# A graph network layer on one Trainium2 core: the source columns of one tile in every 11th group come from TensorE instead of a gather

## The chip, the core and the metric

The kernel runs on one core of one Trainium2 chip. The core has TensorE (PE; its weight loads are listed apart as PEld), VectorE (DVE), ScalarE (ACT), GpSimd (POOL) and SyncE (SP), which issues DMAs. SBUF is the working memory, PSUM the memory into which TensorE writes. The metric is the device time of one execution in microseconds; the time of a kernel is the median of its runs.

## What is computed

One layer of a graph network over 12500 nodes with 64 features and 212500 edges with 32 features. The edges are sorted by their target.

```python
msg_in = jnp.concatenate([nodes[row], nodes[col], edge_features], axis=-1)
messages = _mlp(msg_in, mW1, mb1, mW2, mb2)          # relu(x @ W1 + b1) @ W2 + b2
aggregated = jax.ops.segment_sum(messages, col, num_segments=nodes.shape[0])
upd_in = jnp.concatenate([nodes, aggregated], axis=-1)
return _mlp(upd_in, uW1, ub1, uW2, ub2)
...
x = _layernorm(x + _L0_gnn_ref(x, src, dst, edge_attr_32, ...), axis=-1)
```

Here row is src and col is dst. All numbers are float32.

## The kernel before

The edges go through in 554 groups of 384, a group being three tiles of 128 edges (TG = 3). Group g is worked on in three parts, each of which ends with instructions on other engines:

- *turn* (L373 on): the ring `own.s` holds for every edge of the group the 64 features of its source node and a one-hot row of 32 places, which says to which target in the group's window of 32 nodes the edge goes. Three TensorE transposes (L378) put this into the PSUM tile `ps[0]`, 96 rows by 384 columns. ACT copies it into the block `own.st` (L389), where the edge features have been loaded below it as rows 96 to 127.
- *hidden*: three matmuls (L404) of that block's columns with `wm`, which holds the weights for the source, the window's projected target rows and the weights of the edge features. VectorE applies the relu into `own.h` (L415).
- *sums*: three matmuls (L431) add up the hidden rows by target: the weights are `h`, the moving operand is the one-hot part, repeated TIMES = 4 times, so that 128 columns are streamed, of which the first 32 are used. VectorE adds these to `agg` (L458). After every fourth group, three matmuls (L442) with a column of ones as weights count the edges of each target for all four groups (L463).

In the main loop, step k does turn(k), hidden(k - 2) and sums(k - 4) as one run of TensorE instructions. Only its first instruction waits, for everything that the step needs; only its last reports. PSUM is held twice: groups with an even and an odd number have three banks each, `own.ps[g % 2]`. From time to time a chunk of 512 nodes is finished: its update (L474 to L516) is spread over the steps.

The source features reach `own.s` and `own.st` on two ways. The first is a gather (L167): one indirect DMA of GpSimd for each tile, issued 16 groups ahead. The second is a copy of single columns: `xc` holds the transposed nodes in SBUF, so the features of an edge's source are one column of it, 64 rows by four bytes. For the first tile of 180 marked groups (COPIED) there is no gather; VectorE (20 in each step, L565) and ACT (24 in each step, L567) copy its 128 columns from `xc` straight into `own.st`, at addresses that are held in registers. The addresses are loaded from a list in SBUF (`registers`, L546), which is fetched by SP for eight steps at a time (`indexes`, L525) and turned into byte addresses by VectorE (`addresses`, L531).

The order on each engine is the order of the program text. The dependencies are written out by hand in `after` and `ordered_by_steps`; the tool adds no waits where they say so. A second routine, `unordered`, runs only if the edges aren't sorted as expected, and does not run here.

Of the kernel before, what the change touches and what calls it, by code (L numbers as in the profile page):

```python
# [10 lines left out]
F32 = mybir.dt.float32  # L11
BF16 = mybir.dt.bfloat16
I32 = mybir.dt.int32
# [3 lines left out]
ET = mybir.EngineType  # L17
# [3 lines left out]
P = 128  # L21
# [36 lines left out]
def tiles_of(g):  # L58
# [56 lines left out]
def ordered(ctx: ExitStack, tc: tile.TileContext, a, own, ok):  # L115
# [24 lines left out]
    columned = set(COPIED)  # L140
# [12 lines left out]
    before = {}  # L153

    def ordered_by_steps(i):

# [7 lines left out]
    def gather(g):  # L164
        s = own.s[g % RING]
        loads[g] = [
            nc.gpsimd.indirect_dma_start(  # L167
                out=s[:p, j, :D], out_offset=None, in_=x[:, :],
                in_offset=bass.IndirectOffsetOnAxis(
                    ap=src_sb[:p, g * TG + j : g * TG + j + 1], axis=0),  # L170
            )
            for j, p in enumerate(tiles_of(g)) if j or g not in columned
        ]
        for i in loads[g]:
            after(i, *([turn_by[g - RING]] if g >= RING else []))
# [196 lines left out]
    def turn(g, ps):  # L372


        s = own.s[g % RING]
        xt = ps[0][: D + W, :GE]
        did = [
            nc.tensor.transpose(xt[:, j * P : j * P + p], s[:p, j, :], ident[:p, :p])  # L378
            for j, p in enumerate(tiles_of(g))
        ]  # L380

        def copy(step):
            t, c, n = columns(g)
            turn_by[g] = step
            whole = [(slice(D + W), slice(n))]
            apart = [(slice(D, D + W), slice(P)), (slice(D + W), slice(P, n))]
            copies = [
                ordered_by_steps(
                    after(nc.scalar.activation(t[r, c : c + n][:, m], xt[r, m], AF.Copy), step))  # L389
                for r, m in (apart if g in columned else whole)  # L390
            ]
# [127 lines left out]

    def indexes(i):  # L520

        n = min(SPAN * COLS, P * len(COPIED) - i * SPAN * COLS)
        if n > 0:
            indices[i] = ixp.tile([1, SPAN * COLS], I32, name="index")
            nc.sync.dma_start(indices[i][:, :n], a["src_copied"][:, i * SPAN * COLS :][:, :n])  # L525

    def addresses(i):

        if i in indices:
            t = indices[i][:, : min(SPAN * COLS, P * len(COPIED) - i * SPAN * COLS)]  # L530
            nc.vector.tensor_scalar(t, t, 4.0, float(own.at), ALU.mult, ALU.add)  # L531

    def registers(k, *parts):

        i, n = divmod(k - BEGIN, SPAN)
        if i < 0:
            return
        all_parts = [*((ET.DVE, c) for c in VCOLS), *((ET.Activation, c) for c in ACOLS)]
        for part in parts:
            engine, count = all_parts[part]  # L540
            c0 = (k - BEGIN) * COLS + sum(c for _, c in all_parts[:part])
            count = min(count, P * len(COPIED) - c0)
            if count <= 0:
                return
            b = c0 - i * SPAN * COLS
            _, v = nc.values_load_multi_w_load_instructions(  # L546
                indices[i][0:1, b : b + count], engines=[engine],
                min_val=own.at, max_val=own.at + 4 * (N - 1),
                skip_runtime_bounds_check_because="a source is one of the nodes",
            )  # L550
            held[part] = engine, c0, v

    def fetch(*parts):

        for part in parts:
            engine, c0, v = held.pop(part, (None, 0, ()))
            for q, at in enumerate(v, c0):
# [8 lines left out]
                else:  # L566
                    by[engine] = nc.scalar.activation(o, x_at, AF.Copy)  # L567
                ordered_by_steps(after(by[engine],
                                       *([hidden_by[g - BLOCKS * SB]] if new else [])))

    waiting = [(closes, update(base, p, n)) for base, p, n, closes in PLAN]
    now = []
# [44 lines left out]
    for k in range(G):  # L617
# [67 lines left out]
def unordered(ctx: ExitStack, tc: tile.TileContext, a, own):  # L685
# [30 lines left out]
    nc.sync.dma_start(u2b, a["ub2"][None, :])  # L716

    xT_sb = own.xc[: D + 1, :N]
    nc.vector.memset(xT_sb[D : D + 1, :], 1.0)
    nc.scalar.dma_start(xT_sb[:D, :], a["xT"])  # L720

    ident = const.tile([P, P], F32, name="zident")
    make_identity(nc, ident)
# [269 lines left out]
```

## Time and profile before

| | |
|---|---|
| median of 3 runs | 1875.99 us (1874.75 to 1878.42) |
| the profiled execution | 1872.44 us |
| its span, first to last instruction | 1870.6 us |
| mean granted TensorE clock | 0.952 |
| gathers (L167) | 1481 |
| single columns on VectorE, on ACT (L565, L567) | 10480, 12560 |
| TensorE matmul passes | 9839 |

Busy time is given for each engine by itself. TensorE's matmuls are pipelined: the length that is given for one reaches to the end of its way through the array, so the time that one costs in a row of them is read from start to start. Idle time of an engine is listed with what released it. PEclk is the TensorE clock that was granted, as a share of full speed.

### The profile page before, as it was taken

To read this page: it belongs to the slowest core of one execution; us is meant where nothing else is said; L and a number is where in the kernel's file an instruction comes from. 1 tells how busy PE (TensorE), PEld (TensorE's weight loads), DVE (VectorE), ACT (ScalarE), POOL (GpSimd) and SP (SyncE) were. 2 spreads that over 40 slices of the span, in tenths; PEclk is the share of its full clock that TensorE was granted. 3 is DMA by queue.
4 is the path that set the end of the run, shared out by engine and by line. 5 is a ranking of instruction groups with operands and counts; after the bars stand their busy time and mean duration, and the time that the engine had idled before them with its cause. 6 is when DMAs were issued, how large, how long until landed. Compare 5 with 4: busy or idle time off the path is not lost. (4 is left out here: it accounts for less than half of the span.)

```text
span 1870.6 us, 55967 instructions
## 1 busy us (share of the span) xinstructions
PE 1302.0 (70%) x9839; PEld 1139.3 (61%) x9839; DVE 1452.9 (78%) x13141; ACT 1558.7 (83%) x13374; POOL 1400.1 (75%) x1488
## 2 busy tenths in 40 slices
PE   1777777677767667677676776776767767667676
PEld 0676666666666556566665666665656656556665
DVE  1338888899897888877887878888878888888773
ACT  5249999999998888888888888888888888888871
POOL 7777777777777777777777777777777777777774
PEclk9889999999999998998999998999998999999999
DMA  4543222222222222222222222222222222222221
GB/s 93 138 123 75 54 54 54 51 54 53 52 54 48 50 52 49 50 49 45 54 52 47 52 46 54 48 51 48 53 46 53 45 54 51 48 53 48 50 49 26
DMA packets 112796, 104.10 MB, mean 56 GB/s; under 512 B 51586, under 2 KB 82960, under 8 KB 112432
## 3 DMA queue, kind: packets, MB, share of 16 engines
q0 software_dynamic: 47392, 48.60, 14.8%
q1 hardware_dynamic: 64196, 51.35, 10.0%
q14 instruction: 280, 2.29, 0.4%
q8 instruction: 84, 1.38, 0.3%
q10 hardware_dynamic: 844, 0.48, 0.1%
HBM read 90.61 MB, written 9.62 MB: 54 GB/s over the span
## 5 line engine op out<-in xcount | busy, mean ns | idle before, releaser
L167 POOL DMA_INDIRECT own_s<-in_x,src_sb x1481 | 1399.4, 945 | 452.5 <-issue 342.9
L567 ACT ACTIVATE own_st<-own_xc 64x4 uint8 x12560 | 1265.6, 192 | 60.2 <-issue 52.2
L565 DVE COPY own_st<-own_xc 64x4 uint8 x10480 | 884.5, 190 | 17.3 <-issue 9.2
L378 PE MATMUL own_ps<-own_ident,own_s 128*96 128x128 f32 x1661 | 294.1, 288 | 488.7 <-DMA own_s<-in_x,src_sb 164.0
L378 PEld LDWEIGHTS own_ps<-own_ident,own_s 128*96 128x96 f32 x1661 | 169.1, 131 | 593.5 <-issue 291.0
L431 PE MATMUL own_ps<-own_s,own_h 128*128 128x128 f32 x3322 | 490.3, 287 | 1.2 <-DVE own_h L415 0.6
L404 PE MATMUL own_ps<-own_wm,own_st 128*128 128x128 f32 x3322 | 485.5, 285 | 0.0
L415 DVE TENSOR_SCALAR own_h<-own_ps 128x384 f32<-128x384 f32 x553 | 302.1, 547 | 185.5 <-PE own_ps L442 84.7
L431 PEld LDWEIGHTS own_ps<-own_s,own_h 128*128 128x128 f32 x3322 | 443.3, 203 | 2.3 <-DVE own_h L415 1.2
L404 PEld LDWEIGHTS own_ps<-own_wm,own_st 128*128 128x128 f32 x3322 | 437.8, 201 | 1.8 <-issue 1.2
L389 ACT ACTIVATE own_st<-own_ps 96x384 f32<-96x384 f32 (+2 forms) x734 | 294.2, 401 | 167.5 <-PE own_ps L442 81.6
L458 DVE TENSOR_TENSOR own_agg<-own_ps,own_agg 128x32 f32 x554 | 105.8, 191 | 170.6 <-DVE own_h L415 90.4
L366 DVE TENSOR_TENSOR own_s<-iota,dlc 128x96 f32<-128x96 f32 x554 | 136.2, 247 | 0.3 <-issue 0.2
L442 PE MATMUL own_ps<-own_s,own_one 128*1 128x128 f32 x834 | 120.6, 283 | 0.0
L463 DVE TENSOR_TENSOR own_xc<-own_ps,own_xc 1x32 f32 x554 | 101.9, 184 | 18.5 <-DVE own_xc L463 1.8
L442 PEld LDWEIGHTS own_ps<-own_s,own_one 128*1 128x1 f32 x834 | 60.2, 85 | 35.7 <-issue 3.6
L340 PE MATMUL u_ps<-w1b,own_xc 65*128 65x128 f32 x196 | 33.4, 323 | 58.1 <-ACT t L343 38.8
L340 PEld LDWEIGHTS u_ps<-w1b,own_xc 65*128 65x128 f32 x196 | 29.1, 227 | 62.3 <-ACT t L343 42.1
L343 ACT ACTIVATE t<-u_ps 128x512 f32<-128x512 f32 (+1 forms) x25 | 14.7, 588 | 58.2 <-DMA by_dst<-t 37.9
L487 PE MATMUL u_ps<-same,own_xc 65*128 65x64 f32 (+1 forms) x196 | 37.0, 271 | 1.5 <-ACT u L480 1.4
L489 PE MATMUL u_ps<-u,u 128*128 128x64 f32 (+1 forms) x196 | 38.0, 276 | 0.0
L487 PEld LDWEIGHTS u_ps<-same,own_xc 65*128 65x128 f32 (+1 forms) x196 | 29.7, 191 | 2.3 <-ACT u L480 2.2
(62 smaller groups left out, 257.1 us busy)
## 6 DMA issues: line engine op xcount, KB each, us to landing
own_st<-in_efT SPq DMA_DIRECT2D x138, 192.0 KB
own_s<-in_x,src_sb POOLq DMA_INDIRECT x1481
own_wm<-by_dst SPq DMA_DIRECT2D x554, 16.0 KB
by_dst<-t SPq DMA_DIRECT2D x24, 256.0 KB
out<-o SPq DMA_DIRECT2D x24, 128.0 KB
own_xc<-in_xT SPq DMA_DIRECT2D x12, 179.2 KB
index<-in_src_copied SPq DMA_DIRECT2D x65, 1.4 KB
dlc_i<-in_dst_cols SPq DMA_DIRECT2D x1, 831.0 KB
```

The costliest lines, as they stand in the source:

```text
L167: nc.gpsimd.indirect_dma_start(out=s[:p, j, :D], out_offset=None, in_=x[:, :], in_offset=bass.IndirectOffsetOnAxis(ap=src_sb[:p, g * TG + ...
L366: places_by[g] = nc.vector.tensor_tensor(own.s[g % RING][:, :, D:], iota.unsqueeze(1).to_broadcast([P, TG, W]), dlc[:, g * TG : (g + 1) * ...
L378: nc.tensor.transpose(xt[:, j * P : j * P + p], s[:p, j, :], ident[:p, :p])
L389: after(nc.scalar.activation(t[r, c : c + n][:, m], xt[r, m], AF.Copy), step))
L404: nc.tensor.matmul(pre[:p, j, :], t[:, c + j * P : c + j * P + p], wm[g % NW], start=True, stop=True)
L415: relu_by[g] = [nc.vector.tensor_scalar(h, pre, 0.0, None, ALU.max)]
L431: did.append(nc.tensor.matmul(sg, h[:p, j, :], s[:p, j, D:].unsqueeze(1).to_broadcast([p, TIMES, W]), start=j == 0, stop=j == len(sizes) - 1))
L442: did.append(nc.tensor.matmul(at_ps[:, : len(whole)], own.one, own.ring[:, first_s : first_s + len(whole), j, D:], start=j == 0, stop=j == ...
L458: did = [after(nc.vector.tensor_tensor(agg[:, at], sg[:, 0, :], agg[:, at], ALU.add), step)]
L463: did.append(after(nc.vector.tensor_tensor(count, counted, count, ALU.add), step))
L565: by[engine] = nc.vector.tensor_copy(o, x_at)
L567: by[engine] = nc.scalar.activation(o, x_at, AF.Copy)
```

## The change

In 47 groups, every 11th from group 29 on (BY_PE), the third tile is no longer gathered. Its source columns are copied by TensorE instead, by products with the identity: in each of the 11 steps ahead of such a group, after the step's own matmuls, 12 matmuls (8 in the last step) with `ident[:64, :96]` as weights and one column of `xc` as the moving operand, at an address from a register, write one column each into columns 384 to 511 of the group's PSUM bank, which the transposes leave free. The transposes of a marked group write columns 128 to 511 instead of 0 to 383, so that its third tile lies where the single columns were written. Only the one-hot part of that tile still has to be turned, by a plain matmul of 32 columns with the identity into rows 64 to 95. ACT's copy reads the same number of rows and columns as before.

The 12 addresses of a step are loaded into registers of TensorE ahead of the step's matmuls. The list of addresses has 56 numbers for each step instead of 44. TIMES goes from 4 to 2, so that the sums stream 64 columns. In the routine that does not run, two lines go.

```diff
-TIMES = 4
+TIMES = 2
 BEGIN = 18
 CHECKED = 8
 VCOLS = (12, 8)
 ACOLS = (12, 12)
 COLS = sum(VCOLS + ACOLS)
 SPAN = 8
+PCOLS = 12
+PERIOD = 11
+EACH = COLS + PCOLS
+SIDE = 512 - P
...
+STEPS = G - SHORT - BEGIN
+BY_PE = [g for g in range(BEGIN + PERIOD, G - SHORT, PERIOD)]
+assert PERIOD % 2 == 1 and PCOLS * PERIOD >= P
...
-        tc.declare_no_dep(first.ins, group="quiet", reason="waits for the last of a step")
+        keep = kept if first.ins.engine == ET.PE else []
+        tc.declare_no_dep(first.ins, group="quiet", keep=keep,
+                          reason="waits for the last of a step")
...
-            for j, p in enumerate(tiles_of(g)) if j or g not in columned
+            for j, p in enumerate(tiles_of(g))
+            if (j or g not in columned) and (j < TG - 1 or g not in by_pe)
         ]
...
         s = own.s[g % RING]
-        xt = ps[0][: D + W, :GE]
-        did = [
-            nc.tensor.transpose(xt[:, j * P : j * P + p], s[:p, j, :], ident[:p, :p])
-            for j, p in enumerate(tiles_of(g))
-        ]
+        xt = ps[0][: D + W, 512 - GE :] if g in by_pe else ps[0][: D + W, :GE]
+        did = []
+        for j, p in enumerate(tiles_of(g)):
+            cols = slice(j * P, j * P + p)
+            if j == TG - 1 and g in by_pe:
+                did.append(nc.tensor.matmul(xt[D:, cols], s[:, j, D:], ident,
+                                            start=True, stop=True))
+            else:
+                did.append(nc.tensor.transpose(xt[:, cols], s[:p, j, :], ident[:p, :p]))
...
-        n = min(SPAN * COLS, P * len(COPIED) - i * SPAN * COLS)
+        n = min(SPAN, STEPS - i * SPAN) * EACH
...
+    def loaded(k, offset, count, engine):
+
+        i, n = divmod(k - BEGIN, SPAN)
+        b = n * EACH + offset
+        _, v = nc.values_load_multi_w_load_instructions(
+            indices[i][0:1, b : b + count], engines=[engine],
+            min_val=own.at, max_val=own.at + 4 * (N - 1),
+            skip_runtime_bounds_check_because="a source is one of the nodes",
+        )
+        return v
...
+    def side_columns(k):
+
+        if k < BEGIN:
+            return None
+        n, m = divmod(k - BEGIN, PERIOD)
+        c0, c1 = m * PCOLS, min(P, (m + 1) * PCOLS)
+        if n >= len(BY_PE) or c0 >= c1:
+            return None
+        return BY_PE[n], c0, loaded(k, COLS, c1 - c0, ET.PE)
+
+    def side_fetch(k, work):
+
+        if work is None:
+            return
+        g, c0, v = work
+        for c, at in enumerate(v, SIDE + c0):
+            i = nc.tensor.matmul(own.ps[g % 2][0][: D + W, c : c + 1], ident[:D, : D + W],
+                                 xc_bytes[:D, bass.ds(at - own.at, 4)].bitcast(F32),
+                                 start=True, stop=True)
+            tc.no_tile_sem_insts.add(i.ins.name)
+            tc.add_to_no_dep_group("quiet", i.ins)
+            kept[:] = [i.ins]
...
         if k < G - SHORT:
+            side = side_columns(k)
             between.append(lambda: registers(k, 0))
             step((turn, k), *([(hidden, k - 2)] if k > 1 else []),
                  *([(sums, k - 4)] if k > 3 else []))
+            side_fetch(k, side)
```

More of the change, by code (lines that the diff above doesn't have):

```diff
@@ L151, in after @@
         return first
-    before = {}
+    before, kept = {}, []
     def ordered_by_steps(i):
@@ L540, in registers @@
             engine, count = all_parts[part]
-            c0 = (k - BEGIN) * COLS + sum(c for _, c in all_parts[:part])
+            offset = sum(c for _, c in all_parts[:part])
+            c0 = (k - BEGIN) * COLS + offset
             count = min(count, P * len(COPIED) - c0)
@@ L544, in registers @@
                 return
[L545 to L551, printed above, removed]
+            held[part] = engine, c0, loaded(k, offset, count, engine)
     def fetch(*parts):
@@ L973 @@
         "src": padded(v["src"], NT * P, 0).reshape(NT, P).T,
-        "src_copied": np.concatenate([v["src"][g * GE :][:P] for g in COPIED])[None],
+        "src_copied": np.concatenate(
+            [padded(np.concatenate([v["src"][g * GE :][:P] for g in COPIED]),
+                    STEPS * COLS, 0).reshape(STEPS, COLS),
+             padded(np.concatenate([padded(v["src"][g * GE + GE - P :][:P], PERIOD * PCOLS, 0)
+                                    for g in BY_PE]),
+                    -(-STEPS // PERIOD) * PERIOD * PCOLS, 0).reshape(-1, PCOLS)[:STEPS]],
+            axis=1).reshape(1, -1),
         "dst_cols": padded(v["dst"], G * TG * P, -1).reshape(G * TG, P).T,
```

13 lines of the change are left out of this document (5 added, 8 removed).

## The prediction

> **What bounds the kernel now.** I read the page first, then the DMA-issuing engine, then TensorE step by step, then the granted clock in short windows. Durations are of one profiled execution, 1872.44 us (span 1870.6 us and 1.8 us around it); the median of the three runs, 1875.99 us, is 0.2% above it. The sum is made against 1872.4.
>
> ```profile
> PE 1302.0 (70%) x9839; PEld 1139.3 (61%) x9839; DVE 1452.9 (78%) x13141; ACT 1558.7 (83%) x13374; POOL 1400.1 (75%) x1488
> ...
> L167 POOL DMA_INDIRECT own_s<-in_x,src_sb x1481 | 1399.4, 945 | 452.5 <-issue 342.9
> ```
>
> GpSimd looks only 75% busy, but its 1481 gathers take 1399.4 us and leave 452.5 us of idle in front of them, most of it plain issue: together 1851.9 us, 1.250 us a gather, practically the span. It is never free, so it sets the pace. TensorE has slack; how much is read from the middle of the run, where each step has one turn of three transposes:
>
> ```profile
> 125.00:1796.00 1671.00, 273.08 (x1551) 155.41 (x1551) 0.96 0.24 52
> ```
>
> This is the windows view restricted to line 378: 1551 transposes are 517 steps in 1671.0 us, 3.23 us a step, at a mean granted clock of 0.96. Steps 18 to 534 are those that the change touches. All the rest of the execution is 1872.4 - 1671.0 = 201.4 us.
>
> What TensorE does in a step stands in its timeline (start, length, group):
>
> ```profile
> 904.16 0.51 PE L378 MATMUL own_ps<-own_ident,own_s 128*96 128x128 f32 x3 [1.81 <-ACT own_st L389]
> 904.50 0.83 PE L404 MATMUL own_ps<-own_wm,own_st 128*128 128x128 f32 x6
> 905.17 0.83 PE L431 MATMUL own_ps<-own_s,own_h 128*128 128x128 f32 x6
> 905.93 0.81 PE L442 MATMUL own_ps<-own_s,own_one 128*1 128x128 f32 x6
> ```
>
> Two things are to be seen. A float32 matmul that isn't a transpose is recorded twice: three tiles give x6. Each such pass is one weight load and one matmul, and from start to start a pair costs 0.67 / 6 = 0.112 us. And ahead of the counts of L442, the group of L431 takes 0.76 us instead of 0.67: 0.09 us are lost where the weights change from 128 columns to one.
>
> The two kinds of work that a chunk's update adds, and their number in these 517 steps:
>
> ```profile
> 1705.03 1.02 PE L474 MATMUL u_ps<-own_agg,wc 128*128 128x512 f32 x2
> 1705.89 1.02 PE L475 MATMUL u_ps<-own_xc,ux 97*128 97x512 f32 x2
> 1706.76 0.49 PE L378 MATMUL own_ps<-own_ident,own_s 128*96 128x128 f32 x3
> ...
> 1777.10 0.39 PE L489 MATMUL u_ps<-u,u 128*128 128x64 f32 x2
> 1777.33 0.39 PE L487 MATMUL u_ps<-same,own_xc 65*128 65x64 f32 x2
> 1777.55 0.39 PE L489 MATMUL u_ps<-u,u 128*128 128x64 f32 x2
> ...
> 1778.44 0.39 PE L489 MATMUL u_ps<-u,u 128*128 128x64 f32 x2
> 1779.93 0.50 PE L378 MATMUL own_ps<-own_ident,own_s 128*96 128x128 f32 x3 [1.10 <-DVE own_agg L458]
> 1780.27 0.45 PE L404 MATMUL own_ps<-own_wm,own_st 128*128 128x128 f32 x2
> ...
> L480 ACT ACTIVATE u<-u_ps 128x512 f32<-128x512 f32 x23 | 13.3, 578 | 0.0
> ```
>
> TensorE's work in a mean step: 15 pairs x 0.112 = 1.68; the counts of every fourth step, (6 x 0.109 + 2 x 0.09) / 4 = 0.21; the updates, (4 x 0.43 + 16 x 0.112) x 23 / 517 = 0.16. Sum 2.05 us of 3.23: 1.18 us are free.
>
> **The change, part by part.** *TIMES 4 to 2* (L431 streams 64 columns, not 128). The rows of L487 and L489 have just this form, 64 columns against weights of 128, and still cost 0.22 / 2 = 0.112 us a pair: the weight load sets the spacing. So it saves nothing but some 0.02 us at a step's last matmul; taken as 0. What it does take away is streamed columns, which matters below.
>
> *The removed gathers*: 47 x 1.250 = 58.8 us less on GpSimd. That is a gain only while GpSimd stays the bound.
>
> *The added columns.* In each of the 517 steps TensorE copies 12 columns (8 in the last of eleven), 128 in 11 steps. One column is a matmul with weights ident[:64, :96] and one moving column. The nearest row with one moving column again shows two passes for one call, and short ones, but there the weights have one column too. So the price is that of 96 weight columns, and the last rows with fewer than 128 tell it:
>
> ```profile
> 78.07 0.19 PE L306 MATMUL u_ps<-valid,ones 128*1 128x1 f32 x2 [2.59 <-DVE off L290]
> ...
> 1861.89 0.26 PEld L487 LDWEIGHTS u_ps<-same,own_xc 65*106 65x106 f32 x2 [0.82 <-ACT u L480]
> 1862.07 0.27 PEld L489 LDWEIGHTS u_ps<-u,u 128*106 128x106 f32 x2
> 1862.25 0.35 PEld L487 LDWEIGHTS u_ps<-same,own_xc 65*106 65x106 f32 x2
> ...
> L442 PEld LDWEIGHTS own_ps<-own_s,own_one 128*1 128x1 f32 x834 | 60.2, 85 | 35.7 <-issue 3.6
> ```
>
> Two pairs with 106 weight columns take 0.18 us, 0.09 a pair, against 0.112 with 128; for 96 that gives 0.082 to 0.084. I take 0.084; the bounds are 0.03 (L306, one weight column; two pairs in 0.19 us with their drain) and 0.112. The same weights stand in all of them, but L442 too uses one set of weights throughout and loads it 834 times for 834 matmuls, so nothing spares the reload. 128 x 2 / 11 = 23.3 pairs a step x 0.084 = 1.95 us.
>
> *Going to 64 rows and back*: between 0 (L378 with 96 weight columns to L404 with 128: 0.34 us for three, nothing lost) and twice the 0.09 us seen at L442. I take 0.18, since both the rows and the columns differ. The Trainium skill, "TensorEngine Tiling (Array Packing)", Key Properties, says that a change of tiling mode drains TensorE; the 0.09 us at L442 agrees. By it the 0.18 would stand, without it the step is 4% shorter.
>
> *The registers.* Twelve addresses are loaded on TensorE's queue between the last step's columns and this step's waits.
>
> ```profile
> L546 ACTq TENSOR_LOAD <-index x1047: 549/782/1358, 123.6 to 1814.8; - x175
> ```
>
> On ACT such a load takes at least 0.55 us. Behind it stand the waits and all 15 matmul pairs of the step. While the 1.95 us of columns ahead of it are still queued it costs nothing; if it waits for them, 0.55 us a step. I take 0 and keep 0.55 for the range.
>
> *At nothing*: the third tile of a marked group as a plain matmul, one more pass, 0.112 / 11 = 0.01 us; longer index loads and address arithmetic (352 to 448 numbers, once in eight steps, on SP and DVE), hidden behind TensorE's step, some 0.1 us per eight steps without that cover; writes into the PSUM bank that ACT is reading in every other step, of which no row shows a cost, hidden behind the same step.
>
> Sum for TensorE: 2.05 + 1.95 + 0.18 + 0.01 = 4.19 us a step, against 3.23 that the kernel needs now. TensorE becomes the bound, GpSimd's 58.8 us are worth nothing, and at full clock the time is 517 x 4.19 + 201.4 = 2368 us.
>
> **The clock comes on top.** The granted clock is 0.50 or 1.00, in steps of 3.41 us. Each pair of lines below is one such window and the next one (PE, PEld, DVE, ACT, POOL, then the clock):
>
> ```profile
> 514.12:517.53 3.41, 0.91 (x9) 0.75 (x9) 2.76 (x20) 3.41 (x34) 2.50 (x4) 1.00 0.14 28
> 517.53:520.94 3.41, 3.41 (x19) 3.38 (x18) 3.34 (x38) 2.17 (x18) 2.69 (x3) 0.50 0.16 29
> 520.94:524.36 3.42, 2.60 (x23) 2.44 (x23) 3.29 (x28) 3.42 (x35) 2.62 (x3) 1.00 0.35 70
> ...
> 565.32:568.73 3.41, 1.45 (x13) 1.25 (x12) 2.86 (x24) 3.41 (x35) 2.50 (x4) 1.00 0.34 86
> 568.73:572.14 3.41, 2.69 (x23) 2.56 (x24) 2.44 (x23) 2.07 (x19) 2.65 (x3) 1.00 0.19 37
> ...
> 1777.05:1780.46 3.41, 2.31 (x22) 2.20 (x21) 3.13 (x34) 3.39 (x33) 2.50 (x4) 1.00 0.16 34
> 1780.46:1783.87 3.41, 3.41 (x18) 2.69 (x17) 2.23 (x22) 1.61 (x17) 2.50 (x4) 0.50 0.19 34
> ...
> 1381.10:1384.51 3.41, 2.04 (x18) 1.53 (x16) 2.51 (x24) 3.11 (x28) 2.50 (x4) 1.00 0.17 37
> 1384.51:1387.92 3.41, 1.84 (x15) 1.68 (x15) 3.25 (x30) 3.22 (x31) 2.50 (x4) 1.00 0.12 26
> ```
>
> Nine matmuls in a window and the next is at half clock; thirteen, and it stays at 1.00; after a half-clock window with nineteen the clock returns. But the third pair has 22 matmuls and 2.20 us of weight loads and is throttled, while the fourth, with 18 and only 1.53 us of loads, isn't. The third is the window of the 64-column rows above: fourteen of them (1777.10 to 1778.44, two every 0.22 us), and five of 128. So what counts is streamed columns, not busy time and not weight loads, and the bound lies near 12 matmuls of 128 columns in a window, a 64-column one counting half at most.
>
> Counted so, a step has after the change 3 + 6 + 3 (sums, halved) + 1.5 (counts) + 24 x 23 / 517 = 1.1 (updates) + 0.3 (single columns, second pass) = 14.9, against 17.6 before. In 4.19 us that is 12.1 a window on the mean, just the bound, but it lies in one half of the step: a window that holds the 2.1 us of columns has 1.3 us left, at most 11.6 matmuls. So windows fall below it regularly. At half clock a pair takes 0.22 us and the step 8.4: the mean falls to 6.1. A window with nothing but turns, hidden and sums holds 9 + 3 in 3.2 us, the bare bound; only one with counts or an update, laid right, is clear of it. So the clock mostly stays down. I take 85 of 100 windows at half clock (bounds 70 and 100): the mean rate is 0.575, the step 4.19 / 0.575 = 7.29 us, the time 517 x 7.29 + 201.4 = **3970 us**. With 70 it is 517 x 6.45 + 201.4 = 3536, with 100 it is 517 x 8.38 + 201.4 = 4534.
>
> **The rivals.** *The clock stays up* because TensorE is never idle: 2368 us. For it: the throttled windows above are mostly those with long idle TensorE time. Against it: the window from 1777.05. Its bounds are 2275 (no cost of the mode) and 4.74 us a step, 2652, with the register loads exposed. The Trainium skill, "TensorE: Matmul & The Clock Gate", HAM oscillation, says this: the clock falls after idle gaps of more than about 3.4 us between bursts. This trace shows it fall after the window from 1777.05, whose longest gap is the 1.10 us ahead of L378, so measurement and rule differ here; by the rule the time would be the 2368.
>
> *The columns are cheap*: if the 96-column identity weren't loaded again for each pass, a pair would cost what the one-column rows do, 0.03 us: 2.05 + 0.70 + 0.18 = 2.93 us, under 3.23, GpSimd stays the bound and the time is 1872.4 - 58.8 = 1814 us, faster. The point from which this decides is a pair of 0.043 us ((3.23 - 2.23) / 23.3). Against it: 834 loads of the same weights at L442.
>
> *It does nothing*: a pair of just about that price, with GpSimd's gain given back in waits.
>
> **How the numbers follow.** Half clock most of the time 0.68 (3500 to 4550); clock up 0.24 (2270 to 2650); between the two, the clock falling only at times, 0.02; cheap columns 0.05; nothing 0.01. The likeliest is 3970. Both slower cases are needed for 8 in 10, so the range is 2270 to 4550. What a measurement can tell from no change is about 0.2%; faster 0.05, same 0.01, slower 0.94 are the same cases.
>
> **What would show it.** Right: TensorE busy through the whole span; a group of some 12 000 passes with one moving column and 96-column weights, at 0.08 us a pair in full-clock windows and 0.165 at half; PEclk near 0.55 to 0.6 in the slices; GpSimd idle before gathers for PE; the sums' pairs still 0.112 us apart. Wrong: PEclk near 1.0 with steps of 4.2 us (the clock rule falls), pairs under 0.05 us, or waits of TensorE in front of L378 that are longer than now.

## The result and the profile after

| | before | changed |
|---|---|---|
| median | 1875.78 us (1874.75 to 1878.42, 4 runs) | 3993.56 us (3969.53 to 4011.33, 4 runs) |
| ratio | 1 | 2.128, interval 2.116 to 2.139 |
| profiled execution, its span | 1872.44, 1870.6 us | 3969.53, 3967.8 us |
| mean granted clock | 0.952 | 0.597 |

The kernel takes more than twice its time. The page of the changed kernel, with its busy times, its clock in 40 slices and its costliest groups:

```profile
PE 3706.2 (93%) x21918; PEld 3447.6 (87%) x21918; DVE 1484.3 (37%) x13141; ACT 1641.6 (41%) x13374; POOL 1355.6 (34%) x1441
...
PEclk8656565555556565556555655566656555555557
...
L176 POOL DMA_INDIRECT own_s<-in_x,src_sb x1434 | 1354.8, 945 | 2530.7 <-PE own_ps L445 1459.8
L606 PEld LDWEIGHTS own_ps<-own_xc,own_ident 64*96 64x96 f32 x12032 | 1665.1, 238 | 262.9 <-ACT own_st L403 191.6
L606 PE MATMUL own_ps<-own_xc,own_ident 64*96 x12032 | 1709.3, 271 | 137.3 <-ACT own_st L403 137.3
```

GpSimd and TensorE have changed places. A gather still takes 945 ns, but GpSimd now idles for 2530.7 us in front of its gathers, and most of that ends with TensorE's sums (now L445). TensorE is busy 93% of the span. It makes 21918 passes instead of 9839, and 12032 of them, 47 x 128 x 2, are the added columns (L606). The clock is near one half in nearly every slice. The windows view restricted to the transposes (now L394) gives the length of a step:

```profile
125.50:3900.50 3775.00, 407.64 (x1504) 203.18 (x1504) 0.58 0.10 23
```

3775.0 us over 517 steps are 7.30 us a step, where the step was 3.23. The mean clock of 0.58 means that 84 windows in 100 were at half clock. TensorE's timeline shows three steps, the first two at half clock and the last at full (L418 is hidden, L445 the sums, L456 the counts):

```profile
2001.21 1.38 PE L445 MATMUL own_ps<-own_s,own_h 128*128 128x64 f32 x6
2003.17 4.00 PE L606 MATMUL own_ps<-own_xc,own_ident 64*96 x24 [0.58 <-ACT own_st L403]
2007.10 0.88 PE L394 MATMUL own_ps<-own_ident,own_s 128*96 128x128 f32 x3
2007.77 1.49 PE L418 MATMUL own_ps<-own_wm,own_st 128*128 128x128 f32 x6
2009.05 1.38 PE L445 MATMUL own_ps<-own_s,own_h 128*128 128x64 f32 x6
2010.36 1.44 PE L456 MATMUL own_ps<-own_s,own_one 128*1 128x128 f32 x6
2011.73 4.00 PE L606 MATMUL own_ps<-own_xc,own_ident 64*96 x24
...
2021.26 2.20 PE L606 MATMUL own_ps<-own_xc,own_ident 64*96 x24
2023.38 0.87 PE L394 MATMUL own_ps<-own_ident,own_s 128*96 128x128 f32 x3
2024.05 1.49 PE L418 MATMUL own_ps<-own_wm,own_st 128*128 128x128 f32 x6
2025.33 1.38 PE L445 MATMUL own_ps<-own_s,own_h 128*128 128x64 f32 x6
2026.64 1.59 PE L606 MATMUL own_ps<-own_xc,own_ident 64*96 x16
```

Twelve single columns, 24 passes, take 3.93 us at half clock (2003.17 to 2007.10) and 2.12 us at full clock (2021.26 to 2023.38), which is about as much as all the rest of a step's work. Something else is seen at 2003.17: the columns waited there for ACT's copy L403. From the sums to the columns it is 1.96 us in that step, and 1.31 us (2025.33 to 2026.64) in a step without the wait. The waits view puts that wait beside the others:

```profile
POOL own_s L176 <- PE own_ps L445: 1459.8, 380, 6.2
...
PE own_ps L606 <- ACT own_st L403: 137.3, 216, 0.8
...
PE own_ps L394 <- DMA own_s<-in_x,src_sb: 29.2, 36, 1.0
```

The columns are written into the PSUM bank of the marked group. In every step whose own group has the same parity (five of eleven), ACT is copying out of that bank, so the first column carries a wait for the copy; 216 times it is seen.

The clock can be followed window by window. Columns: PE, PEld, DVE, ACT, POOL, then the clock.

```profile
2020.01:2023.42 3.41, 3.41 (x28) 2.40 (x27) 2.09 (x23) 2.82 (x25) 2.10 (x3) 1.00 0.09 19
2023.42:2026.84 3.42, 3.42 (x18) 3.28 (x17) 0.09 (x1) 0.09 (x1) 0.00 (x0) 0.50 0.06 14
2026.84:2030.25 3.41, 3.41 (x33) 3.02 (x33) 2.25 (x23) 2.84 (x25) 1.89 (x2) 1.00 0.33 85
2030.25:2033.66 3.41, 3.41 (x36) 3.34 (x36) 2.68 (x26) 2.83 (x25) 2.37 (x3) 1.00 0.11 26
2033.66:2037.08 3.42, 3.42 (x20) 3.39 (x19) 0.87 (x6) 0.11 (x2) 0.46 (x1) 0.50 0.08 17
```

In the windows from 2020.01 and from 2030.25 TensorE is busy all the time, and yet the next one is at half clock. The first holds the single columns from 2021.26, the second holds 64-column passes and the single columns from 2032.12: both are full of passes that load many weights and stream little. Counted in matmuls of 128 streamed columns by 128 rows, they hold 8.7 and 6.5. The window from 2023.42 has only 18 passes, but they are sums, hidden and turns, 11.9 such matmuls, and after it the clock returns. The Trainium skill, "TensorE: Matmul & The Clock Gate", HAM oscillation, ties the throttle to idle gaps of more than about 3.4 us; these rows have no gap and are throttled, so the measurement decides.

### The profile page after: what moved, and what is told of

Its sections match the earlier page's. It is cut to its first block, busy times and chain, and to the rows that moved or that the text cites. A ratio compares the mean times of both kernels' runs of the same rounds, so it can differ in the third digit from the quotient of the medians.

```text
span 3967.8 us, 86395 instructions
## 1 busy us (share of the span) xinstructions
PE 3706.2 (93%) x21918; PEld 3447.6 (87%) x21918; DVE 1484.3 (37%) x13141; ACT 1641.6 (41%) x13374; POOL 1355.6 (34%) x1441
## 4 chain that ended last, share of the span: by engine, by line
issue 42%; PE 33%; POOL 21%; DMA 2%; ACT 1%; DVE 1%; ACTq 0%; POOLq 0%; SPq 0%; DVEq 0%
POOL own_s L176 21%; PE own_ps L606 14%; PE own_ps L418 6%; PE own_ps L445 6%; PE own_ps L394 4%; PE own_ps L456 2%; ACT own_st L403 1%; DMA own_s<-in_x,src_sb 1%; DMA by_dst<-t 1%; PE u_ps L350 0%; PE u_ps L501 0%; PE u_ps L503 0%; PE u_ps L488 0%; ACT own_agg L277 0%; ACT own_xc L216 0%
## 5 line engine op out<-in xcount | busy, mean ns | idle before, releaser
L176 POOL DMA_INDIRECT own_s<-in_x,src_sb x1434 | 1354.8, 945 | 2530.7 <-PE own_ps L445 1459.8
L606 PEld LDWEIGHTS own_ps<-own_xc,own_ident 64*96 64x96 f32 x12032 | 1665.1, 238 | 262.9 <-ACT own_st L403 191.6
L606 PE MATMUL own_ps<-own_xc,own_ident 64*96 x12032 | 1709.3, 271 | 137.3 <-ACT own_st L403 137.3
L403 ACT ACTIVATE own_st<-own_ps 96x384 f32<-96x384 f32 (+2 forms) x734 | 297.9, 406 | 2060.5 <-PE own_ps L445 1309.4
L418 PE MATMUL own_ps<-own_wm,own_st 128*128 128x128 f32 x3322 | 754.1, 392 | 0.0
L445 PEld LDWEIGHTS own_ps<-own_s,own_h 128*128 128x128 f32 x3322 | 720.7, 312 | 6.1 <-DVE own_h L429 4.4
L445 PE MATMUL own_ps<-own_s,own_h 128*128 128x64 f32 x3322 | 719.0, 384 | 3.8 <-DVE own_h L429 2.8
L418 PEld LDWEIGHTS own_ps<-own_wm,own_st 128*128 128x128 f32 x3322 | 696.4, 302 | 20.1 <-issue 15.8
L394 PE MATMUL own_ps<-own_ident,own_s 128*96 128x128 f32 x1614 | 429.1, 396 | 55.7 <-DMA own_s<-in_x,src_sb 29.2
L394 PEld LDWEIGHTS own_ps<-own_ident,own_s 128*96 128x96 f32 x1614 | 217.7, 170 | 71.8 <-issue 42.5
L456 PE MATMUL own_ps<-own_s,own_one 128*1 128x128 f32 x834 | 179.5, 378 | 0.0
L456 PEld LDWEIGHTS own_ps<-own_s,own_one 128*1 128x1 f32 x834 | 77.6, 106 | 58.4
```

The lines of the kernel that those rows point to most:

```text
L176: nc.gpsimd.indirect_dma_start(out=s[:p, j, :D], out_offset=None, in_=x[:, :], in_offset=bass.IndirectOffsetOnAxis(ap=src_sb[:p, g * TG + ...
L394: did.append(nc.tensor.transpose(xt[:, cols], s[:p, j, :], ident[:p, :p]))
L418: nc.tensor.matmul(pre[:p, j, :], t[:, c + j * P : c + j * P + p], wm[g % NW], start=True, stop=True)
L445: did.append(nc.tensor.matmul(sg, h[:p, j, :], s[:p, j, D:].unsqueeze(1).to_broadcast([p, TIMES, W]), start=j == 0, stop=j == len(sizes) - 1))
L456: did.append(nc.tensor.matmul(at_ps[:, : len(whole)], own.one, own.ring[:, first_s : first_s + len(whole), j, D:], start=j == 0, stop=j == ...
L606: i = nc.tensor.matmul(own.ps[g % 2][0][: D + W, c : c + 1], ident[:D, : D + W], xc_bytes[:D, bass.ds(at - own.at, 4)].bitcast(F32), start ...
```

## The experiments

Theory A, the prediction's: TensorE is the bound because each pass reloads 96 weight columns, and the clock falls because a window streams too little. Its rivals: the price lies in the width or rows of the single columns or in the rest of the change, and the clock follows something else. Four kernels (TIMES = 2 in the kernel before, TIMES = 4 in the changed one, more columns streamed, fewer weight columns) ran together at a time when the kernel before took 2432.22 us (2422.77 to 2434.59) at a clock of about 0.84. Their clocks and start-to-start times can be compared with the changed kernel's; their absolute times are safe to compare only with each other. All the others ran beside a kernel before of 1872.8 to 1874.7 us.

**The same kernel again.**

> The changed kernel itself, beside the others of this call, since the chip of the last four runs took 2432 us for the kernel before instead of 1876. Where the kernel before takes 1876 us: 3970 to 4010 us. Where it takes 2432 us: TensorE is the bound either way, so 3950 to 4200 us, with the same 0.085 and 0.160 us a pair.

4016.9 us at a clock of 0.587, with the same start-to-start times. The kernel before took 1873.18 us beside it, so the doubling is the kernel's and not that of one occasion.

**The change without the single columns.** In place of the 128 columns there is one matmul of 128 fixed columns for each marked group; the copying itself is left out, and the register loads go with it.

```diff
-        for c, at in enumerate(v, SIDE + c0):
-            i = nc.tensor.matmul(own.ps[g % 2][0][: D + W, c : c + 1], ident[:D, : D + W],
-                                 xc_bytes[:D, bass.ds(at - own.at, 4)].bitcast(F32),
-                                 start=True, stop=True)
+        if c0 == 0:
+            i = nc.tensor.matmul(own.ps[g % 2][0][: D + W, SIDE:], ident[:D, : D + W],
+                                 own.xc[:D, :P], start=True, stop=True)
```

> The changed kernel without the single columns: one matmul of 128 fixed columns stands for each marked group, so those tiles carry wrong features. Everything else of the change stays: 47 gathers fewer, TIMES = 2, the other place in PSUM, the address lists and the register loads on TensorE. Theory A (GpSimd was the bound, and only the columns cost): 1876 - 58.8 = 1817 us where the kernel before takes 1876, a ratio of 0.97. Rival (the rest of the change costs too, by register loads ahead of a step or by a lower clock with TIMES = 2): ratio 1.00 or more.

Unlike what was expected, the register loads on TensorE aren't in its trace either, so they can't be a cost here. The median was 1887.39 us (two runs at 1867, four from 1885 to 1893.35), 1.0085 of before (interval 1.0064 to 1.0106), with the clock at 0.87 to 0.89. The page's row for GpSimd in the profiled run, one of the two short ones with 1867.75 us:

```profile
L176 POOL DMA_INDIRECT own_s<-in_x,src_sb x1434 | 1356.1, 946 | 445.0 <-issue 364.6
```

Two things follow. Of the 2118 us that the change costs, the single columns with their loads and waits make 2106. And the rest isn't free either: GpSimd's 1434 gathers now add up to 1801 us (1356.1 + 445.0), some 50 less than before, but the kernel isn't faster. Its last gather ends 50.8 us earlier than before, at 1802.6 instead of 1853.4 us of the span, but TensorE's last transposes start 48.7 us after that, where it was 2.4 us before: TensorE's steps fall behind the gathers, while the clock fell from 0.95 to 0.88. The same kernel with the sums at 128 columns again (TIMES = 4) tells what:

> The run without the single columns (the marked groups' third tiles carry wrong features, as there) once more, with TIMES = 4. That run's ratio was 1.0085 although GpSimd had 47 gathers fewer, and its clock 0.88. Theory A (TIMES = 2 alone lowers the clock, and at half clock TensorE's steps are too long): the clock returns to 0.95 or more and most of the 58.8 us appears, ratio 0.97 to 0.985. Rival (the register loads or the gathers' own gaps keep it there): ratio 1.00 or more with the clock up.

```profile
L176 POOL DMA_INDIRECT own_s<-in_x,src_sb x1434 | 1357.1, 946 | 438.1 <-issue 326.4
```

1824.69 us (1819.28 to 1832.64), 0.9747 of before (0.9715 to 0.978), at a clock of 0.93. The last transposes now start 11.5 us after the last gather. So TIMES = 2 alone costs 1887.4 - 1824.7 = 63 us here, without removing or adding a single pass. Without it the 47 gathers give 48 of the 58.8 us that 47 x 1.250 promised.

**TIMES alone, in the kernel before** (`TIMES = 2` instead of 4, nothing else):

> The kernel before with TIMES = 2 alone. Theory A: 14.6 instead of 17.6 matmuls of 128 columns a step of 3.23 us is 15.4 a window on the mean, unevenly spread, so a third of the windows fall under 12: mean clock 0.78 to 0.88 instead of 0.952; the time stays within 1% of 1876 us, since TensorE has slack and GpSimd sets the pace. Theory B: the clock stays near 0.95 and the time at 1876 us.

Beside the kernel before of 2432.22 us it took 2451.88 us (2441.8 to 2458.44), a ratio of 1.0085 (1.0055 to 1.0114), and the clock went from 0.84 to 0.76. **TIMES = 4 in the changed kernel:**

> The changed kernel with TIMES back at 4. Theory A (the clock is granted by the columns that the matmuls stream in a window, about 12 matmuls of 128 columns): a step streams 17.9 instead of 14.9 matmuls of 128 columns, so fewer windows fall under the bound: mean clock 0.65 to 0.75 instead of 0.597, time 3250 to 3550 us, although no pair gets shorter. Theory B (the clock goes by something else, such as the many small instructions, or it does not matter): the pairs of the sums stay 0.112 us apart, nothing else changes, 3970 to 4010 us and a clock of 0.60.

3689.72 us at a clock of 0.684, with the single columns at 0.085 and 0.160 us as before. The windows view of L394 in it:

```profile
125.50:3620.00 3494.50, 372.45 (x1534) 188.14 (x1534) 0.67 0.13 27
```

With the 47 tiles that a plain matmul turns (L391, not in this row) the 1534 transposes are 1581 / 3 = 527 steps of 6.63 us. The clock came out as Theory A had it, the time didn't fall as far as the 3250 to 3550 us that were expected: a faster clock shows what half clock had hidden. In 102 of the 464 steps with 24 single-column passes TensorE stands idle between the columns and the next transposes, in the changed kernel in 65. In all of them but one the columns had waited for ACT's copy. There the load of the next addresses starts 1.87 us after the first column, in steps without that wait 0.68 us after it (medians, at full clock), and the transposes start 0.31 us after the load's end: 3.04 us after the columns instead of 2.13. So the wait for the bank is what brings the address load into the open. All three comparisons say that streamed columns carry the clock.

**More columns streamed per single column.** Each source column is repeated side by side up to 96 times; later columns overwrite the copies, so the result stays.

```diff
+WIDE = 96
...
-            i = nc.tensor.matmul(own.ps[g % 2][0][: D + W, c : c + 1], ident[:D, : D + W],
-                                 xc_bytes[:D, bass.ds(at - own.at, 4)].bitcast(F32),
-                                 start=True, stop=True)
+            n = min(WIDE, 512 - c)
+            i = nc.tensor.matmul(
+                own.ps[g % 2][0][: D + W, c : c + n], ident[:D, : D + W],
+                xc_bytes[:D, bass.ds(at - own.at, 4)].bitcast(F32).to_broadcast([D, n]),
+                start=True, stop=True)
```

> The changed kernel, each single column streamed up to 96 times side by side (as far as the bank reaches, 60 on the mean); the copies to the right of its own place are overwritten by the next ones. The same number of passes and weight loads. Theory A: streaming is free beside the weight load of 96 columns at full clock, and the columns of a step stream some 11 matmuls of 128 columns more: clock 0.75 to 0.9, time 2700 to 3250 us, with half-clock windows where the bank's end leaves only few columns. Theory B: more work for TensorE, the time stays at 3990 us or grows.

3862.1 us, clock 0.657: a miss. So I sorted every window of the profiled runs by what it streamed. Count for each pass its streamed columns, divide by 128, lay this evenly over the pass's recorded length, and say that a window of less than 11.9 is followed by half clock. That misplaces 8 of 532 windows of the kernel before, 23 of 1146 of the changed kernel, 18 of 1049 with TIMES = 4, 17 of 686 in the kernel before with TIMES = 2 and 28 of 1064 in the next kernel. Here, however, it misplaces 245 of 1100; with the copied columns left out it is 150, and with each of them counted half, 23. These are columns of 64 rows, where most other passes use 128. So a streamed column seems to count by the share of the rows it uses, and this run had only half the cover that I had given it. The later runs bear that out: if every pass counts by its rows, the same bound misplaces 4 of 829 windows of the kernel with all three edits below, whose columns have 96 rows, against 56 without the rows, and 119 of the 11075 windows of all fourteen profiles, against 484. Weight loads don't sort them: in the changed kernel the best bound on the weight columns loaded misplaces 203 of 1146, and to call every window one before half clock would misplace 209.

**Fewer weight columns.** All 96 rows of `xc`, but 64 weight columns, which write the 64 rows that are needed.

```diff
-            i = nc.tensor.matmul(own.ps[g % 2][0][: D + W, c : c + 1], ident[:D, : D + W],
-                                 xc_bytes[:D, bass.ds(at - own.at, 4)].bitcast(F32),
+            i = nc.tensor.matmul(own.ps[g % 2][0][:D, c : c + 1], ident[: D + W, :D],
+                                 xc_bytes[: D + W, bass.ds(at - own.at, 4)].bitcast(F32),
```

> The changed kernel with 64 weight columns instead of 96 for a single column (the identity's first 96 rows and 64 columns; the column comes with the 32 constant rows below it, which meet zeros). Theory A (the weight load sets the spacing of these pairs): 0.058 instead of 0.085 us at full clock and 0.107 instead of 0.160 at half; 23.3 pairs save 0.62 to 1.24 us a step, and a shorter step also lifts more windows over the bound: 3250 to 3550 us. Theory B (a pair costs what two passes cost to issue, with addresses from registers): spacing and time unchanged, 3990 us.

3699.61 us, clock 0.586. Its timeline:

```profile
2007.86 2.72 PE L606 MATMUL own_ps<-own_xc,own_ident 96*64 x24
2010.51 0.87 PE L394 MATMUL own_ps<-own_ident,own_s 128*96 128x128 f32 x3
```

24 passes in 2.65 us at half clock, 0.110 each, against 0.164 (3.93 / 24) with 96 weight columns: two thirds, as 64 is of 96, although the rows went up from 64 to 96. So weight columns set the price. The Trainium skill, "TensorE: Matmul & The Clock Gate", LDWEIGHTS (loading the stationary operand), says the same, that the load goes by columns and not by rows. The time stayed above the 3250 to 3550 us that were expected: against the 3993.56 us of the changed kernel, taken at another time, it is 294 / 517 = 0.57 us a step, not 3.93 - 2.65 = 1.28. Part of the gap is again the address load: in the 144 half-clock steps whose columns had waited for ACT's copy, the transposes came 3.03 us after the columns and not 2.65. With those the columns take 2.63 us of a mean step where they took 3.34, so 0.71 us is what they gave; the rest was not split up.

**All three at once**: TIMES = 4, 64 weight columns on 96 rows, each source column repeated up to 64 times.

```diff
-TIMES = 2
+TIMES = 4
+WIDE = 64
...
+            n = min(WIDE, 512 - c)
+            i = nc.tensor.matmul(
+                own.ps[g % 2][0][: D, c : c + n], ident[: D + W, : D],
+                xc_bytes[: D + W, bass.ds(at - own.at, 4)].bitcast(F32).to_broadcast(
+                    [D + W, n]),
```

> The changed kernel with all 47 groups, but TIMES = 4, 64 weight columns for a single column, its moving column streamed 64 times side by side (less near the bank's end), and 96 rows of it instead of 64. In the run with 96 copies and 64 rows the clock rose only to 0.657; its windows are told apart best when a streamed column of 64 rows counts one half. If rows count, these columns count 0.75 each and give some 7 matmuls of 128 columns a step more: clock over 0.95, pairs 0.058 us, a step of 2.05 + 23.3 x 0.058 + 0.16 and the wait for ACT's copy in every other step, 3.6 to 4.0 us: 2070 to 2350 us. If rows don't matter and the columns were simply worth little: clock under 0.8, over 2700 us.

2886.73 us, clock 0.895. The clock rose, though not to the 0.95 where I had put it, and the time stayed far above the 2070 to 2350 us. The timeline and, of the registers, the time of each address operation on TensorE's sequencer, PEldq (ns min/median/max, first and last start; ACTq below is ACT's):

```profile
1503.33 1.92 PE L608 MATMUL own_ps<-own_xc,own_ident 96*64 x24
1505.25 0.50 PE L395 MATMUL own_ps<-own_ident,own_s 128*96 128x128 f32 x3
...
1507.67 2.12 PE L608 MATMUL own_ps<-own_xc,own_ident 96*64 x24 [0.57 <-ACT own_st L404]
1510.69 0.70 PE L395 MATMUL own_ps<-own_ident,own_s 128*96 128x128 f32 x3 [0.90 <-DVE own_st L585]
```

```profile
L552 PEldq TENSOR_LOAD <-index x517: 587/847/1392, 119.3 to 2810.2; - x173
...
L608 PEldq FUSED_REGOPS  x6016: 82/85/103, 120.8 to 2813.4; - x195
```

The wait for ACT's copy and the load of twelve addresses, 0.85 us, both stand in the open. At 1507.67 the columns start 0.57 us late, and 0.90 us lie idle after them, about one load. The row names a DVE copy there, but in 212 of the 213 steps whose 24 passes had waited for ACT's copy TensorE is idle until 0.32 us (median) after the load's end and then starts the transposes, so it is the load. From the columns to the transposes it is 3.06 us in such steps at full clock and 1.88 us in the others, 2.45 us on the mean, where the columns need 1.54 in the kernel below that loads its addresses later, their address arithmetic (12 x 0.085 = 1.02 us) included. A step takes 5.22 us at a mean clock of 0.894; if all of it went by the clock, 5.22 x 0.894 = 4.67 us would be left at full clock and a time of 517 x 4.67 + 201.4 = 2616 us. That is an estimate, and a low one, since waits don't shrink with the clock; it is well above rival 1's 2368 us.

**Columns only in the steps that have room.** Every 23rd group, 11 columns in every other step, which are the steps whose own group uses the other bank; the rest as in the kernel above.

```diff
-PCOLS = 12
-PERIOD = 11
+PCOLS = 11
+PERIOD = 23
...
-        c0, c1 = m * PCOLS, min(P, (m + 1) * PCOLS)
-        if n >= len(BY_PE) or c0 >= c1:
+        c0 = m // 2 * PCOLS
+        c1 = min(P, c0 + PCOLS)
+        if n >= len(BY_PE) or m % 2 or c0 >= c1:
```

> As the last one, but with every 23rd group only (22 groups, 22 gathers fewer) and 11 columns in every other step, in those in which ACT copies from the other bank. Theory A: TensorE needs 2.05 us in one step and 2.05 + 22 x 0.058 + 0.16 = 3.49 us in the next, 2.77 on the mean, under 3.23, and nothing waits for ACT's copy; GpSimd stays the bound and wins 22 x 1.25 = 27 us: ratio 0.985 to 0.995 where the kernel before takes 1876 us. Rival (TensorE's long step delays its followers, the clock falls, or the register loads stand in the way): ratio 1.00 to 1.05.

3051.17 us (3049.49 to 3058.17), ratio 1.630 (1.627 to 1.633), far outside both ranges. Neither TensorE (68% busy) nor GpSimd (45%) is the bound. The register loads are:

```profile
L552 ACTq TENSOR_LOAD <-index x1047: 771/2592/3316, 123.9 to 2994.7; - x175
L552 PEldq TENSOR_LOAD <-index x264: 1059/2633/3309, 120.1 to 2889.0; - x132
```

ACT's own load of 12 addresses, twice a step, in which nothing was changed, takes 2.59 us in the median instead of 0.78. What changed is where the list of a step starts: it has 44 + 11 = 55 numbers of four bytes, so that only every fourth step starts at a multiple of 16 bytes, counted from the list's start. With 12 columns it has 56, as in the changed kernel, and every start is such a multiple. That is the only edit of the next run (`PCOLS = 12`):

> The run with every 23rd group, with 12 columns in a loading step instead of 11 and nothing else: the address list has 56 numbers a step instead of 55, so each load begins at a multiple of 16 bytes again. In that run the loads of 12 numbers took 2.59 us on ACT at the median, against 0.78 in all the others. If the place in memory is the cause: loads back at 0.78 to 0.85 us, time 1870 to 2100 us. If the number of columns or their place among the steps is the cause: about 3050 us again.

```profile
L552 ACTq TENSOR_LOAD <-index x1047: 542/782/1252, 127.4 to 1814.5; - x175
L552 PEldq TENSOR_LOAD <-index x242: 589/848/1040, 122.6 to 1751.4; - x121
```

1866.81 us in one run: 1184 us for one number more in the list. Which multiple decides, the trace of the slow run tells: there ACT's loads took 0.79 us (median of 262) in every fourth step, the one at a multiple of 16 bytes, and 2.60 us (785) in the steps that were 4, 8 or 12 bytes off. ACT's two loads of a step begin 48 bytes apart and were both fast in the former, so a multiple of 32 isn't needed.

Last, the address load is moved behind the step's own matmuls, where nothing of the step queues behind it but the columns themselves:

```diff
-            side = side_columns(k)
             between.append(lambda: registers(k, 0))
...
-            side_fetch(k, side)
+            side_fetch(k, side_columns(k))
```

> The last one (every 23rd group, 12 columns in every other step) with the addresses loaded behind the step's own matmuls instead of ahead of them, as in the run with every 33rd group. GpSimd has 22 x 1.25 = 27.5 us less to do. TensorE needs 2 x 2.05 + 12 x 0.163 + 0.16 + some 0.3 = 6.5 us in two steps, just the 6.46 that there are. Theory A (the exposed load of up to 0.85 us kept the last run at 1867 us): ratio 0.985 to 0.993. Rival (TensorE is already full at 12 columns, wherever the load stands): ratio 0.995 to 1.005.

1847.71 us (1847.02 to 1848.33), 0.9851 of before (0.9835 to 0.9868), and 19 us under the kernel with the load ahead, which ran once, on another chip. The page and the timeline:

```profile
PE 1648.1 (89%) x15493; PEld 1481.0 (80%) x15493; DVE 1454.6 (79%) x13141; ACT 1553.8 (84%) x13374; POOL 1382.5 (75%) x1466
...
L177 POOL DMA_INDIRECT own_s<-in_x,src_sb x1459 | 1381.7, 947 | 445.8 <-issue 341.7
```

```profile
1002.84 0.83 PE L446 MATMUL own_ps<-own_s,own_h 128*128 128x128 f32 x6
1003.60 1.61 PE L609 MATMUL own_ps<-own_xc,own_ident 96*64 x24
1005.14 0.53 PE L395 MATMUL own_ps<-own_ident,own_s 128*96 128x128 f32 x3
...
1006.18 0.83 PE L446 MATMUL own_ps<-own_s,own_h 128*128 128x128 f32 x6
1006.95 0.51 PE L395 MATMUL own_ps<-own_ident,own_s 128*96 128x128 f32 x3
```

GpSimd sets the pace again, 1381.7 + 445.8 = 1827.5 us for 1459 gathers, 1.253 each, with idle time that is mostly issue. The 27.0 us that are won are the 22 gathers that went (22 x 1.250 = 27.5). Every other step has 1.54 us of columns, the clock is 0.97, and by the page all idle time of TensorE ahead of the columns adds up to 22.1 us. This kernel beats both the kernel before and the changed one. The same with 8 columns, a period of 33 and so 15 gathers less:

> Every 33rd group (15 groups), 8 columns in every other step, those in which ACT copies from the other bank; 64 weight columns, 96 rows, up to 64 copies side by side, TIMES = 4; the 8 addresses are loaded behind the step's own matmuls on TensorE's queue, not ahead of them. TensorE needs 2 x 2.05 + 8 x 0.163 + 0.16 + some 0.3 of exposed load = 5.9 us in two steps, against 6.46. Theory A: GpSimd stays the bound and wins 15 x 1.25 = 19 us, ratio 0.985 to 0.995. Rival (any long TensorE step is paid in full by its followers): ratio 1.00 to 1.03.

1855.79 us (1853.53 to 1857.86), 0.9913 (0.9896 to 0.9929): 17.0 us for 15 x 1.250 = 18.8.

## Why the prediction was right, and where its terms were off

- **TensorE becomes the bound, GpSimd's gain is worth nothing**: right. GpSimd idles for the sums (1459.8 us), and in the kernel without the columns its idle time is mostly issue again.
- **One column costs a load of 96 weight columns, 0.084 us**: right, 2.12 / 24 = 0.088 at full clock with the change back to 128 rows in it. The rival of cheap columns fell with it. At half clock I took 0.168; it is 0.164.
- **TIMES 4 to 2 saves nothing and takes streamed columns away**: right. The sums' six passes still take 1.28 to 1.31 us at half clock; at the end of a step, from the sums to the columns, it saves 0.05 us at full clock (0.71 against 0.76 with TIMES = 4), not 0.02. The two pairs of kernels above put the loss on the clock.
- **The clock counts streamed columns, with the bound near 12 of 128 in a window, and falls in 85 of 100 windows**: right, 84. "A 64-column one counting half at most" held, but a further thing I had no row for: rows count too. With one streamed column per pass this didn't touch the sum; it did decide the copied-columns experiment.
- **8.38 us for a step at half clock**: the sum is near the mark, its terms less so. Start to start at half clock, most often: transposes 0.66, hidden 1.28, sums 1.31, columns 3.93 x 23.3 / 24 = 3.82, counts 1.37 / 4 = 0.34, and 0.32 of updates taken at twice the predicted 0.16: 7.73 us. The change to 64 rows and back was the largest surplus: 0.36 us predicted at half clock, about 0.12 seen, 0.03 going (1.31 - 1.28) and 0.09 coming back (3.93 - 24 x 0.160). The kernel with 64 weight columns on 96 rows shows the same (1.31, and 2.65 - 24 x 0.107 = 0.08), so it isn't a price of the 64 rows alone. The plain matmul of the marked tile was taken too low: from these transposes to hidden it is 0.69 us instead of 0.37 at full clock, 0.32 / 11 = 0.03 us a step and not 0.01.
- **"Writes into the PSUM bank that ACT is reading ... of which no row shows a cost"**, taken as 0: wrong in size, and wrong as a picture. The program doesn't write while ACT reads; it waits. That costs 0.65 us at half clock (1.96 - 1.31) in the 216 of 517 steps that show the wait, 0.27 us a mean step; and in full-clock steps it also brings the address load into the open, as the next point says. The Trainium skill, "PSUM — Partial Sum Buffer", PSUM bank collisions raise a hardware error, asks for just such a guard, by bank and not by address; what would happen without it no run here shows. Idle time before the transposes adds 55.7 us by their page row, 0.11 us a step. 7.73 + 0.27 + 0.11 = 8.11 against 8.38: the surplus and the forgotten wait partly cancel. This isn't yet the measured step: 8.11 us of half clock would be 8.11 x 0.5 / 0.58 = 6.99 us at the mean clock, and it was 7.30. Weighted with the clock, a step's work is 7.30 x 0.58 = 4.2 us, the 4.19 of the prediction, but the terms above make only 8.11 / 2 = 4.06 of it. The rest is time that doesn't shrink at full clock, the columns' above all, which take 2.04 us on this scale and not 3.82 / 2 = 1.91. So the clock was rightly sized (0.58 against 0.575), but that the 4.19 fits too, and 3970 came so near to 3993.56, is partly luck.
- **The register load at 0, with 0.55 us kept for the range**: right at half clock, where 3.93 us of columns cover it, and in full-clock steps whose columns start at once (2.13 us to the transposes, nothing idle). It shows in the 65 of 464 steps, wholly or partly at full clock, whose columns had waited for ACT's copy: 2.98 us. With the clock up and narrower weights it is the rule: 2.45 us on the mean instead of 1.54 in the three-edits kernel, 0.9 us a step, more than the 0.55 us of the upper bound. The prediction looked at the load and at the bank each by itself and missed that the second delays the first.
- **Rival 1, 2368 us with the clock up**: did not happen, and was itself too low. The three-edits kernel has narrower weights than the change and still took 2886.73 us at a clock of 0.895, since wait and load lie open there. Its upper bound of 2652 held a load of 0.55 us, not the wait.
- **"Waits of TensorE in front of L378 longer than now"**, named as a sign of error: they are shorter (55.7 us). The new wait stands in front of the columns instead.

## What to carry to other kernels

An idle engine takes extra work for nothing only up to its idle time per step: here 1.18 us on TensorE, which holds 24 passes of 64 weight columns in every other step, not 24 of 96 in each. Price such work by passes times weight columns, look at what it waits for (the bank it writes, the addresses it needs), and look at what it does to the clock: here passes with few streamed columns, or few rows, kept an engine busy and its clock low. An operand repeated for width that looks wasteful, like TIMES = 4, may be what holds the clock up; before cutting it, count the streamed columns of a 3.41 us window, each by the share of the rows in use.

## What the runs showed of the hardware that was not expected

- Loading 12 numbers into ACT's registers took 0.79 us in the median where a step's list began at a multiple of 16 bytes and 2.60 us where it began 4, 8 or 12 bytes off, both in the same trace. A kernel of 1866.81 us, with every list in place, became one of 3051.17 with three lists of four out of place.
- The clock's count of streamed columns goes by the rows in use: 64 of 128 rows counted half (23 of 1100 windows misplaced, against 245 and 150 for full and none). The rule was read off this run, with a bound of 11.9 matmuls fitted to the windows; in the later run with 96 rows, counted as 0.75, it misplaces 4 of 829.
- A column at an address in a register costs TensorE's sequencer 0.085 us of address arithmetic, as much as one of its two passes at full clock.
- At one time the kernel before took 2432 us and not 1875. The profile taken then, of the kernel before with TIMES = 2, has register loads of the same medians as elsewhere (0.78 and 0.84 us) and this wait. All four traces of that time have waits for "remote", and none of the other ten:

```profile
POOL own_s L167 <- remote: 248.2, 156, 9.0
```

What "remote" was there stays open, and so does whether it belongs to a chip: the four runs and the next four carry the same chip number, and beside the latter the kernel before took 1873.18 us.
